# The gate's last product, made whole behind its own block or by quarters inside the next one

## The chip, the core and the metric

One core of a Trainium2 chip runs the whole kernel. The metric is the device time of one execution in microseconds (us), given as the median of several runs. Traces are of one profiled execution each; times inside a trace are counted from the first instruction of the span.

## What is computed

The layer takes x of shape 8 x 256 x 512 and returns `x + s * g`. `xn` is x with each row normalized; `s` is a latent attention over xn, `g` is the silu of a small FFN over the same xn:

```python
xn = _layernorm(x, axis=-1)
s = _L0_attn_ref(xn, ...)                      # 128 heads, latent 64, rope part 64
gate = silu(_qlora_linear(xn, w1q, a1, b1))    # 512 -> 1376
up = _qlora_linear(xn, w3q, a3, b3)
g = silu(_qlora_linear(gate * up, w2q, a2, b2))  # 1376 -> 512
x = x + s * g

def _qlora_linear(x, wq, A, B):
    w = jnp.tile(wq, (1, 4))
    return x @ w.T + (x @ A.T @ B.T) * 0.5
```

The weights `wq` are tiled four times along the input. So the input can be folded, its four quarters summed, before it meets the weight. For the last product this means that the 1376 hidden features are folded to 344 ahead of the product with `w2q`. The low-rank part (A, then B) is carried along as two further rows of the folded input.

## The kernel before

The kernel has two phases. The first (`first_phase`, about the first 217 us of the trace) normalizes x, makes the small projections that attention needs and the whole FFN, and stores the gates `g` in DRAM. The second is attention. All instructions are issued in the order written: nothing reorders them across a queue, and each engine works its queue off in that order. PSUM tiles come from one pool of eight banks (`bank`), each reused when the engines have done with it.

The first phase goes over four token blocks `tb` of 512 tokens (L674). For each block:

- Six steps `u` (L676) call `main(tb, u)`, which handles two of the eleven hidden chunks (one in the last step). For each chunk TensorE makes `px` and `py`, four matmuls of 32 x 512 each (`on_columns`, L169). VectorE adds the low-rank part (L541 and L545), ScalarE applies silu (L544), and the product gate times up is made on GpSimd (L558) or VectorE (L551, L552, L556). The gate tiles have two buffers.
- `fold` (L560) sums the four quarters of the hidden features on GpSimd (L570 to L572) into `h4`, in three parts; parts 1 and 2 come behind step 5. `low_out` (L574) makes the low-rank part `pm2` on TensorE. Its third call finishes it: ScalarE (L592) and three VectorE instructions (L594) write it into rows 96 to 127 of the third part of `h4`.
- If there is a next block, its transposes come in step 4, and behind step 5 come `sums` (L474: L479 on VectorE, L480 on GpSimd, L481 on VectorE), `narrow` (TensorE `pm`, then L497 on VectorE and copies L505 on ScalarE), the third `low_out` of this block, and `down` (TensorE `pp`). VectorE's L594 stands behind L481 and L497 in its queue, and L480 behind the folds in GpSimd's.
- `gate_out(tb)` (L598, called at L711) makes the last product. For each of four tiles of 128 tokens, a bank `pf` collects three parts k of `h4` times `w2_sb`, each four matmuls. The order is: parts 0 and 1 of all four tiles, then part 2 of all four. Part 2 is the one that waits for L594. ScalarE then takes each bank with a silu into a tile `gs` (L608; two buffers), and SyncE's queue stores it (L609), 256 KB each.
- Behind it come a set-up (tb = 0 only) and the statistics of the block after the next (`norm`, L715: VectorE L416 to L430, GpSimd L440 to L450). ScalarE's `norm_one` uses them in the steps of the next block.

`h4` has one buffer. The last block (tb = 3) has pieces of attention's projections (`Project`, L679) placed in its steps 2 to 5, and preparations (`between`) behind each step; there `gate_out(3)` is the last work on TensorE before attention begins.

The core of the last product before the change:

```python
for ks in ((0, 1), (2,)):
    for n in range(4):
        for k in ks:
            on_columns(
                pfs[n], h4s[tb][:, k, ds(n * P, P)], w2_sb[:, k, :], k == 0, k == 2
            )
```

Of the kernel before, what the change touches and what calls it, by code (L numbers as in the profile page):

```python
# [37 lines left out]
def mla_ffn_gate_kernel(  # L38
# [60 lines left out]
    def bank(name):  # L99
        return ps_all.tile([P, 512], F32, tag="b", name=name)  # L100
# [68 lines left out]
    def on_columns(to, w, x, start, stop):  # L169

        for t in range(4):
            tile_ = slice(32 * t, 32 * t + 32)
            nc.tensor.matmul(to[tile_], w[:, tile_], x, start=start, stop=stop, skip_group_check=True)  # L173
# [140 lines left out]
    def first_phase(between):  # L314
# [16 lines left out]
        def load_x(tb):  # L331
            xts[tb] = []
            for n in range(4):
                t = f1.tile([P, D], F32, tag="xt", name=f"xt_{tb}_{n}", bufs=6)
                nc.sync.dma_start(out=t, in_=x[ds(tb * TB + n * P, P), :])
                xts[tb].append(t)
# [116 lines left out]
        def norm_one(tb, n, mv, rstd, off):  # L453
            xns[tb] = xts[tb]
            xn, one = xts[tb][n], rstd[:, n : n + 1]
            if tb:
                nc.scalar.activation(xn, xn, AF.Identity, bias=off[:, n : n + 1], scale=one)
            else:
                nc.vector.tensor_scalar(xn, xn, mv[:, n, 0:1], one, ALU.subtract, ALU.mult)

        def turn(tb):
            a = f1.tile([P, KT, TB], F32, tag="act1", name=f"act1_{tb}")
            xnT[tb] = a
            for n in range(4):
                pt = bank(f"xpt_{tb}_{n}")
                for c in range(KT):
                    nc.tensor.transpose(pt[:, ds(c * P, P)], xns[tb][n][:, ds(c * P, P)], ident)
                pt = pt.rearrange("p (c s) -> p c s", c=KT)
                if tb or n % 2 == 0:
                    nc.scalar.copy(a[:, 0:KT, ds(n * P, P)], pt)  # L470
                else:
                    nc.vector.tensor_copy(a[:, 0:KT, ds(n * P, P)], pt)
# [38 lines left out]
        def down(tb):  # L511
            c = f1.tile([P, TB], F32, tag="tmp", name=f"c_{tb}")
            nc.scalar.copy(c, over_xn(tb, "pp", wdn_sb))
            nc.sync.dma_start(out=cs_d[tb], in_=c)
            sum_x(tb, xnT[tb])
# [3 lines left out]
        def pair(u):  # L519


            return [2 * (i % 4) + i // 4 if i < 8 else i for i in range(2 * u, min(2 * u + 2, NCH))]

        def place(c):
            return 4 * (c % 2) + c // 2 if c < 8 else c

        def main(tb, u):

            n = u // 2
            if u % 2 == 0:  # L530
                hTs[tb, n] = f2.tile([P, 4, TB], F32, tag="hT", name=f"hT_{tb}_{n}")
            h = hTs[tb, n]
            chunks = pair(u)
            gates, ups = [], []
            for i, c in enumerate(chunks):
                px, py = (bank(f"p{'xy'[k]}_{tb}_{u}_{i}") for k in range(2))
                on_columns(px, w1_sb[:, c], xsum[tb][0], True, True)
                on_columns(py, w3_sb[:, c], xsum[tb][1], True, True)
                gates.append(f2.tile([P, TB], F32, tag="gate", name=f"gate_{tb}_{u}_{i}"))
                ups.append((py, h[:, c // 2, :] if c < 8 and (tb or u > 1) and (i == 0 or u in (0, 2)) else py))  # L540
                nc.vector.scalar_tensor_tensor(  # L541
                    gates[i], lows[tb][0], bcol_sb[:, place(c), 0:1], px, ALU.mult, ALU.add
                )
                nc.scalar.activation(gates[i], gates[i], AF.Silu)  # L544
                nc.vector.scalar_tensor_tensor(  # L545
                    ups[i][1], lows[tb][1], bcol_sb[:, place(c), 1:2], py, ALU.mult, ALU.add
                )
            for c, gate, (py, up) in zip(chunks, gates, ups):
                if c >= 8:
                    m = c - 8  # L550
                    nc.vector.tensor_mul(h[0:96, m, :], gate[0:96], py[0:96])  # L551
                    nc.vector.tensor_mul(  # L552
                        h[32 * m : 32 * m + 32, 3, :], gate[96:128], py[96:128]
                    )
                elif up is py:
                    nc.vector.tensor_mul(h[:, c // 2, :], gate, py)  # L556
                else:
                    nc.gpsimd.tensor_mul(up, gate, up)  # L558

        def fold(tb, n):  # L560

            rows = CH[n][1]
            h = hTs[tb, n]
            if n == 0:
                h4s[tb] = f1.tile([P, 3, TB], F32, tag="h4", name=f"h4_{tb}")
            if n == 2:
                nc.gpsimd.memset(h4s[tb][64:96, n, :], 0.0)
            h4 = h4s[tb][:rows, n, :]
            h4b = f1.tile([P, TB], F32, tag="h4b", name=f"h4b_{tb}_{n}")
            nc.gpsimd.tensor_add(h4, h[:rows, 0, :], h[:rows, 1, :])  # L570
            nc.gpsimd.tensor_add(h4b[:rows], h[:rows, 2, :], h[:rows, 3, :])  # L571
            nc.gpsimd.tensor_add(h4, h4, h4b[:rows])  # L572

        def low_out(tb, n):  # L574


            rows = CH[n][1]
            h = hTs.pop((tb, n))
            if n == 0:
                mid2ps[tb] = bank(f"pm2_{tb}")  # L580
            for q in range(4):
                nc.tensor.matmul(
                    mid2ps[tb][32 * q : 32 * q + 32, :],
                    a2_sb[:rows, q, n, :],
                    h[:rows, q, :],
                    start=(n == 0),
                    stop=(n == 2),
                )
            if n == 2:
                m2 = mid2ps.pop(tb)  # L590
                to = h4s[tb][96:128, n, :]
                nc.scalar.mul(to, m2[0:32], 0.5)  # L592
                for q in range(1, 4):
                    nc.vector.scalar_tensor_tensor(  # L594
                        to, m2[32 * q : 32 * q + 32], 0.5, to, ALU.mult, ALU.add
                    )

        def gate_out(tb):  # L598
            pfs = [bank(f"pf_{tb}_{n}") for n in range(4)]
            for ks in ((0, 1), (2,)):  # L600
                for n in range(4):
                    for k in ks:
                        on_columns(
                            pfs[n], h4s[tb][:, k, ds(n * P, P)], w2_sb[:, k, :], k == 0, k == 2
                        )
            for n in range(4):
                gs = f2.tile([P, D], F32, tag="gs", name=f"gs_{tb}_{n}")
                nc.scalar.activation(gs, pfs[n], AF.Silu)  # L608
                nc.sync.dma_start(out=gates_d[4 * tb + n], in_=gs)  # L609
# [64 lines left out]
        for tb in range(NTB):  # L674
            more = tb + 1 < NTB
            for u in range(6):  # L676
                pj = None
                if not more and u >= 2:
                    pj = Project(u - 2)  # L679
                    pj.start()  # L680
                main(tb, u)
                if pj:
                    pj.second()
                    pj.end()
                if u in (3, 5):
                    fold(tb, u // 2 - 1)
                    low_out(tb, u // 2 - 1)
                if u == 1 and tb == 0:
                    stats = norm(1)
                if more:  # L690
                    for n in range(4):
                        if u == (n if tb else 2 + n // 2):
                            norm_one(tb + 1, n, *stats)
                if u == 4 and more:
                    turn(tb + 1)
                if u == 1 and tb + 2 < NTB:
                    load_x(tb + 2)
                if tb == NTB - 2 and u == 1:
                    between(1)
                if u == 5:  # L700
                    fold(tb, 2)
                if not more:
                    between(u + 2)
            if more:
                sums(tb + 1)
                narrow(tb + 1)
                low_out(tb, 2)
                down(tb + 1)
            else:
                low_out(tb, 2)  # L710
            gate_out(tb)  # L711
            if tb == 0:
                between(0)
            if tb + 2 < NTB:
                stats = norm(tb + 2)  # L715
# [42 lines left out]
    def between(step):  # L758
# [25 lines left out]
        else:  # L784
# [3 lines left out]
            load_act(3)  # L788

    first_phase(between)  # L790


# [330 lines left out]
```

## Time and profile before

| what | value |
|---|---|
| median of 3 runs | 1985.15 us (1983.88 to 1985.93) |
| the profiled execution's own time | 1985.59 us |
| its span, first to last instruction | 1983.8 us |
| mean granted TensorE clock | 0.998 |
| busy share of the span: TensorE, VectorE, ScalarE, GpSimd | 99%, 79%, 55%, 38% |
| first `px` of block 0, 1, 2, 3 | 23.61, 69.69, 113.17, 155.57 us |
| first score matmul of attention behind `gate_out(3)` | 217.01 us |

The profile names engines PE (TensorE), DVE (VectorE), ACT (ScalarE), POOL (GpSimd), and SPq for the DMA queue that SyncE issues into. In a timeline a row has the start, the duration, the engine, the line of the code, the operation, what it writes and reads, and how many instructions were merged; in square brackets is the idle time just ahead of it and what ended it. Each four matmuls of `on_columns` appear as eight records. Matmuls overlap, so their pace is read from the starts of successive groups: `px` at 113.17 us, `py` at 114.03, `px` at 114.89 make 0.86 us for four matmuls of 512 columns. A table by windows gives, for stretches of time, each engine's busy time and the number of instructions, the granted TensorE clock (PEclk; 1.00 is full speed), and the DMA share.

### The profile page before, as it was taken

Reading aid. Unit: us, or ns where it says so; the run is one execution under the profiler, and the core shown is the slowest. Engines: PE = TensorE matmul, PEld = TensorE weight load, DVE = VectorE, ACT = ScalarE, POOL = GpSimd, SP = SyncE. Lnnn points to the kernel's source line nnn. Section 1 sums busy time; section 2 is a strip of 40 time slices with the busy share of each in tenths; the row PEclk is TensorE's granted clock in tenths of the full one; section 3 lists DMA queues with packets and bytes.
Section 4 is the critical chain, followed back from the end, with each engine's and each line's share of the span. In section 5 each row is a group of like instructions: output and inputs, shape, how many; then the busy total and the mean of one; then the engine's idle time right before and its main releaser. Section 6 shows DMA issues by size and latency. Waiting matters only on the chain.

```text
span 1983.8 us, 86720 instructions
## 1 busy us (share of the span) xinstructions
PE 1966.9 (99%) x38065; PEld 1401.4 (71%) x38065; DVE 1571.2 (79%) x2666; ACT 1091.4 (55%) x2987; POOL 759.1 (38%) x1113
## 2 busy tenths in 40 slices
PE   8999999999999999999999999999999999999998
PEld 4334577777777767777777767777777767777776
DVE  7764678888787877788787877788787877888788
ACT  3333556556556555556556555556556555556654
POOL 5876545554552323232232323232332323232231
PEclk9999999999999999999999999999999999999999
DMA  6235322222232223221232223221232222222212
GB/s 195 100 118 184 109 88 87 88 69 85 88 129 74 100 87 111 91 87 66 87 117 76 100 87 108 93 88 66 88 115 77 100 87 86 83 88 84 70 56 71
DMA packets 120049, 187.53 MB, mean 95 GB/s; under 512 B 10716, under 2 KB 84844, under 8 KB 119674
## 3 DMA queue, kind: packets, MB, share of 16 engines
q1 hardware_dynamic: 119665, 181.97, 26.8%
q8 instruction: 301, 4.93, 1.0%
q14 instruction: 75, 0.61, 0.1%
q10 hardware_dynamic: 8, 0.02, 0.0%
HBM read 147.86 MB, written 34.10 MB: 92 GB/s over the span
## 4 chain that ended last, share of the span: by engine, by line
PE 91%; POOL 3%; DVE 3%; issue 2%; DMA 1%; ACT 0%; SPq 0%; POOLq 0%; ACTq 0%; DVEq 0%
PE q L173 40%; PE sc L824 34%; PE av L870 11%; PE po L173 2%; PE pf L173 1%; PE qq L249 1%; DVE pt L853 1%; POOL hT L558 1%; POOL h4b L571 0%; DVE nmx L837 0%; POOL h L570 0%; PE py L173 0%; DMA xt<-in_x_dram 0%; PE px L173 0%; POOL h L572 0%
## 5 line engine op out<-in xcount | busy, mean ns | idle before, releaser
L843 ACT ACTIVATE pr<-sc,nmx 128x256 f32<-128x256 f32 x2048 | 814.4, 500 | 471.8 <-DVE nmx L837 469.0
L837 DVE TENSOR_REDUCE nmx<-sc 128x2 f32<-128x512 f32 x1024 | 635.6, 683 | 288.9 <-PE sc L824 264.8
L853 DVE STREAM_TRANSPOSE pt<-pr 128x512 f32<-128x512 f32 x1024 | 635.1, 678 | 0.0
L216 POOL TENSOR_TENSOR e<-e,e 128x256 f32<-128x256 f32 x128 | 93.8, 733 | 1043.8 <-ACT e L211 558.2
L173 PE MATMUL q<-x,ws 128*32 128x256 f32 x8192 | 488.9, 379 | 0.2 <-POOL ws L137 0.2
L824 PE MATMUL sc<-act,qr 32*128 32x256 f32 x8192 | 488.6, 374 | 0.0
L824 PEld LDWEIGHTS sc<-act,qr 32*128 32x128 f32 x8192 | 421.0, 185 | 21.9 <-issue 0.2
L173 PEld LDWEIGHTS q<-x,ws 128*32 128x32 f32 x8192 | 266.1, 110 | 176.3 <-POOL ws L137 0.6
L173 PE MATMUL q<-x,w 128*32 128x256 f32 x6144 | 381.6, 381 | 0.7 <-DVE py L545 0.7
L173 PEld LDWEIGHTS q<-x,w 128*32 128x32 f32 x6144 | 187.0, 110 | 155.8 <-ACT pr L843 35.9
L824 PE MATMUL sc<-kc,qcm 32*128 32x256 f32 x4096 | 280.9, 387 | 0.0
L870 PE MATMUL av<-pt,vpad 128*32 128x128 f32 x8192 | 236.4, 273 | 1.9 <-ACT pr L843 1.2
L870 PEld LDWEIGHTS av<-pt,vpad 128*32 128x32 f32 x8192 | 226.4, 110 | 14.5 <-issue 3.0
L824 PEld LDWEIGHTS sc<-kc,qcm 32*128 32x128 f32 x4096 | 198.2, 184 | 51.9 <-issue 39.4
L211 ACT COPY e<-q 128x256 f32<-128x256 f32 x512 | 202.3, 396 | 25.5 <-PE q L173 25.3
L890 ACT ACTIVATE acc<-av,sides_sb 128x256 f32<-128x256 f32 (+1 forms) x130 | 54.2, 469 | 246.6 <-PE av L870 246.6
L269 POOL TENSOR_TENSOR qcm<-qc,mask_sb 128x1024 f32<-128x1024 f32 x64 | 122.3, 1911 | 0.0
L217 POOL TENSOR_TENSOR e<-e,e 128x256 f32<-128x256 f32 x128 | 93.6, 732 | 10.0
L218 POOL TENSOR_TENSOR qr<-e,e 128x256 f32<-128x256 f32 x128 | 93.6, 731 | 10.1
L310 POOL COPY vpad<-vall 32x128 f32<-32x128 f32 x256 | 74.9, 292 | 10.7 <-PE av L870 2.7
L228 DVE TENSOR_TENSOR qr<-e,q 128x256 f32<-128x256 f32 x128 | 53.9, 421 | 22.5 <-POOL e L216 17.0
L541 DVE SCALAR_TENSOR_TENSOR gate<-low,bcol_sb,px 128x512 f32<-128x512 f32 x44 | 32.8, 745 | 43.6 <-POOL hT L558 24.5
(124 smaller groups left out, 1134.5 us busy)
## 6 DMA issues: line engine op xcount, KB each, us to landing
w<-in_w_rope_dram SPq DMA_DIRECT2D x128, 512.0 KB
ws<-sums_d SPq DMA_DIRECT2D x96, 512.0 KB
sums_d<-ws SPq DMA_DIRECT2D x32, 512.0 KB
x<-xs_d SPq DMA_DIRECT2D x28, 256.0 KB
xt<-in_x_dram SPq DMA_DIRECT2D x16, 256.0 KB
xs_d<-xt SPq DMA_DIRECT2D x16, 256.0 KB
gate_d<-gs SPq DMA_DIRECT2D x16, 256.0 KB
g<-gate_d SPq DMA_DIRECT2D x16, 256.0 KB
```

Source lines behind the costliest of these rows:

```text
L173: nc.tensor.matmul(to[tile_], w[:, tile_], x, start=start, stop=stop, skip_group_check=True)
L211: nc.scalar.copy(self.e[i], self.banks[i])
L216: nc.gpsimd.tensor_add(m6, m6, m1)
L217: nc.gpsimd.tensor_add(m7, m7, m6)
L218: nc.gpsimd.tensor_add(self.out(1, 1), self.split(m7), self.split(m5))
L269: nc.gpsimd.tensor_mul(qcm, qks[b, sg // 2][0].rearrange("p (q i) -> p q i", i=32).unsqueeze(2).to_broadcast([P, 8, 4, 32]), mask_sb[:, ds ...
L310: nc.gpsimd.tensor_copy(vpad[rows, :, :, 8 * t + 4 * (sg % 2) :][..., :4], valls[b][rows, :, sg])
L824: nc.tensor.matmul(sc[r][:, h, :], lhs.rearrange("p t i -> p (t i)"), rhs, start=(part == 0 and h == 0), stop=(part == 2), skip_group_chec ...
L837: nc.vector.tensor_reduce(nmx[:, r, :], scs[n, f][r], AX.X, ALU.max, negate=True)
L843: nc.scalar.activation(p[:, h, :], scs[n, f][r][:, h, :], AF.Exp, bias=nmxs[n, f][:, r, h : h + 1])
L853: nc.vector.transpose(pts[n, f // 2, r].rearrange("p k q i -> p q k i")[:, ds(2 * (f % 2), 2)], prs.pop((n, f, r)).rearrange("p h (k j) -> ...
L870: nc.tensor.matmul(av[32 * r : 32 * r + 32, ds(half * P, P)], vpad[:, k, r, :], pt[r][:, k].rearrange("p q i -> p (q i)"), start=(k == 0), ...
```

## The change

`gate_out` takes the list of tiles that it makes. For blocks 0 to 2 it is no longer called behind the block. In its place, each of the steps u = 0 to 3 of the next block calls it for one tile, in front of that step's `main`. For the last block it stays where it was, with all four tiles.

```diff
-        def gate_out(tb):
-            pfs = [bank(f"pf_{tb}_{n}") for n in range(4)]
+        def gate_out(tb, tiles):
+            pfs = {n: bank(f"pf_{tb}_{n}") for n in tiles}
             for ks in ((0, 1), (2,)):
-                for n in range(4):
+                for n in tiles:
                     for k in ks:
                         on_columns(
                             pfs[n], h4s[tb][:, k, ds(n * P, P)], w2_sb[:, k, :], k == 0, k == 2
                         )
-            for n in range(4):
+            for n in tiles:
                 gs = f2.tile([P, D], F32, tag="gs", name=f"gs_{tb}_{n}")
                 nc.scalar.activation(gs, pfs[n], AF.Silu)
                 nc.sync.dma_start(out=gates_d[4 * tb + n], in_=gs)
@@
                     pj = Project(u - 2)
                     pj.start()
+                if tb and u < 4:
+                    gate_out(tb - 1, [u])
                 main(tb, u)
@@
             else:
                 low_out(tb, 2)
-            gate_out(tb)
+                gate_out(tb, range(4))
             if tb == 0:
                 between(0)
```

On TensorE's queue the order at a block's end was: `pp`, parts 0 and 1 of tiles 0 to 3 (32 matmuls), part 2 of tiles 0 to 3 (16 matmuls), then the next block's first `px`. Now it is: `pp`, parts 0, 1, 2 of tile 0 (12 matmuls), the next block's four products of step 0, then 12 matmuls of tile 1, step 1, and so on. ScalarE's four silus and SyncE's four stores of a block move with them; the orders on VectorE and GpSimd are the same as before.

## The prediction

> **What bounds the kernel now.** I read the page first: PE is busy almost all the time at full clock, so what counts is PE's time and any hole in it.
>
> ```profile
> span 1983.8 us, 86720 instructions
> PE 1966.9 (99%) x38065; PEld 1401.4 (71%) x38065; DVE 1571.2 (79%) x2666; ACT 1091.4 (55%) x2987; POOL 759.1 (38%) x1113
> ```
>
> The change touches only the first 217 us, so I next cut that stretch at the first `px` of blocks 1, 2, 3 and at attention's first matmul (table by windows: PE, PEld, DVE, ACT, POOL busy, granted clock, DMA).
>
> ```profile
> 69.69:113.17 43.48, 41.90 (x412) 14.72 (x408) 30.12 (x49) 17.00 (x28) 31.84 (x44) 1.00 0.33 115
> 113.17:155.57 42.40, 41.38 (x413) 14.63 (x408) 26.57 (x38) 17.01 (x28) 29.31 (x35) 1.00 0.39 132
> 155.57:217.01 61.44, 59.89 (x908) 26.23 (x900) 26.43 (x41) 19.57 (x42) 47.23 (x57) 1.00 0.42 148
> ```
>
> PE holds the pace here too; the holes are small. Then the timelines around the ends of blocks 0 and 1, PE first.
>
> ```profile
> 58.98 7.05 PE L173 MATMUL pf<-w_sb,h 128*32 128x512 f32 x64
> 66.26 2.31 PE L173 MATMUL pf<-w_sb,h 128*32 128x512 f32 x17 [0.23 <-issue]
> ...
> 102.39 7.05 PE L173 MATMUL pf<-w_sb,h 128*32 128x512 f32 x64
> 109.74 3.64 PE L173 MATMUL pf<-w_sb,h 128*32 128x512 f32 x32 [0.30 <-DVE h L594]
> 113.17 1.07 PE L173 MATMUL px<-xs,w_sb 128*32 128x512 f32 x8
> ```
>
> The 64 records of parts 0 and 1 run while part 2 is not ready; part 2 starts as soon as L594 is done. DVE's rows say when that is, and why:
>
> ```profile
> 64.01 2.14 DVE L594 SCALAR_TENSOR_TENSOR h<-pm,h 32x512 f32<-32x512 f32 x3 [1.99 <-ACT h L592]
> ...
> 98.05 1.10 DVE L479 TENSOR_TENSOR xs<-act 128x512 f32<-128x512 f32 x1
> 102.92 1.76 DVE L481 TENSOR_TENSOR xs<-xs,xs 128x512 f32<-128x512 f32 x1 [3.77 <-POOL xs L480]
> 107.46 2.14 DVE L594 SCALAR_TENSOR_TENSOR h<-pm,h 32x512 f32<-32x512 f32 x3 [1.99 <-ACT h L592]
> ```
>
> So part 2 comes at the end of a chain: folds on POOL, L480, L481, L497, copies on ACT, L594. The long first piece of `gate_out` is what PE does meanwhile. Last, ACT, where the old order has its cost:
>
> ```profile
> 118.98 1.23 ACT L608 ACTIVATE gs<-pf 128x512 f32<-128x512 f32 x2 [6.65 <-DMA gate_d<-gs]
> 120.23 1.15 ACT L544 ACTIVATE gate<-gate 128x512 f32<-128x512 f32 x2
> ```
>
> The third `gs` waits 6.65 us for a buffer still being stored. The silus of step 0 stand behind it, then POOL's products, then VectorE's step 1.
>
> **What moves, on PE.** Nothing is added: 12 groups (0.86 us each, 10.3 us) per block either way. What changes is what stands ahead of the part that waits.
>
> Block 0 to 1: up to `pp` all is as before, so L594 ends at 66.15 as before. PE has done tile 0's parts 0 and 1 (16 records at 0.107 us, 1.72) at 60.70, and must then wait to 66.26 with everything queued behind: tiles 1 to 3, and step 0's `px`. Hole 5.56 us, where 0.41 was lost (58.98 + 6.87 = 65.85). The first `px` comes at 67.12 instead of 69.69, but three tiles (7.72 us) are still owed.
>
> Block 1: PE's work to the next wait is 0.86 (tile 0, part 2), 13.7 (steps 0 to 3, 16 groups), 7.7 (tiles 1 to 3), 3 `low_out` 2.6, step 4 3.4, transposes 2.2, step 5 1.7, `pm` 3.5, `pp` 3.4, tile 0's parts 0 and 1 1.7: 40.8. No wait is in sight: the silus of step 0 no longer stand behind the stores, and VectorE's step 1 starts at 77.8 (POOL's set-up ends at 76.45, plus one 1.3 us product), 2 us earlier than before. So PE is there at 66.26 + 40.8 = 107.05. L594: PE now reaches step 3 late, `px` of step 4 goes at 89.4, and VectorE follows PE. Step 4 on VectorE starts at 90.5 (89.59 before), its four products end at 96.65, and step 5's end at 99.5 (98.02 before). POOL's second add of the last fold (L571) waits for that: 99.55 + 1.72, L572 and L480 to 103.85 (102.88 before). From L480 to L594 it was 102.88 to 109.60, 6.72 us; so L594 ends at 110.6. Hole 3.6 us, where 0.48 was lost. The next `px` is at 111.5 (113.17 before).
>
> Block 2 has no set-up, but the same PE pace from step 2 on: again 44.4 us from hole end to hole end, 110.7 to 155.0, hole 3.6 us (0.45 before), first `px` of block 3 at 155.9 (155.57 before).
>
> Block 3 then has 7.72 us more PE work than before.
>
> The sum: holes 5.56 + 3.6 + 3.6 = 12.8, less the 1.3 lost there now: +11.4. What the change gives back: block 1 took 43.48 for 40.8 of work, 2.6 lost, of which 0.48 is in the hole: 2.1 (waits for banks behind `gs` and behind the late VectorE). Block 2: 42.40 for 40.6, less 0.45: 1.35. Block 3: `py` at 161.97 waits for `gs`, and `q` at 167.40 for L545, 0.9 each; I take 1.5. Together 5.0. Net +6.4 us.
>
> **Other queues.** ACT: silus of a tile are 0.60 us, one per step, and ACT is under half busy there: hidden; the second one waits behind `norm_one` for POOL's offsets to 77.3 in block 1, but the bank it frees is wanted at 80.8. SP: four stores per block, 0.5 to 1.3 us of issue each. The loads of x for the block after the next, and in block 2 the loads of rope weights, now stand behind two stores instead of four, so not later. In block 3, tile 1's store stands behind the two stores of `ws`, which wait for POOL (168.7 and 171 before); the silu that needs its buffer is wanted near 186. Were that cover gone, tile 3's silu would be late and a bank with it: 3 us at most. Banks: `pf` now is one of five per step, not four; in block 3, with `Project`'s four, nine are wanted of eight, and the ninth takes a bank that ACT has copied out by then: between the last of `Project`'s first products and that group lie 2.6 us of `pf` and three groups, 5 us of PE work. No gain is seen there and at most 1 us of loss; I take 0. After attention starts nothing moves relative to `gate_out(3)`; PE has no slack there (its waits of over 0.3 us behind 217 us sum to under 2 us), so the shift arrives whole at the end.
>
> **The rule that weighs.** No PE wait in this trace is longer than 1.7 us behind the first 12 us, so no row shows what a 5.56 us hole does to the clock. The nearest rows are at the start: the clock falls in 8.5 to 9.0 and comes back at about 15.5, almost 7 us at half, although PE idles only 1.45 us there (its earlier work was transposes and two-row products).
>
> ```profile
> 8.50:9.00 0.50, 0.50 (x2) 0.70 1.01 286
> 9.00:9.50 0.50, 0.50 (x2) 0.50 1.24 217
> 15.00:15.50 0.50, 0.50 (x12) 0.50 0.31 86
> 15.50:16.00 0.50, 0.50 (x16) 0.97 0.85 225
> ```
>
> The Trainium skill, "TensorE: Matmul & The Clock Gate", section "Why this matters for your kernels", asks for no idle gaps over about 3 us between bursts, since an idle window puts the clock to half until a busy one has passed; Part 1 gives a free-running window of about 3.4 us. By the rows of full speed alone a hole costs only itself (+6.4). By the rule, a drop costs one window at half, an estimate of 1.7 us (up to 3.4 if it lasts the 7 us of the start's rows). A hole of 5.56 holds an empty window in (5.56 - 3.4)/3.4, some 60 cases of 100 and more if a nearly empty one is enough; a hole of 3.6 seldom. I take one drop, at the first hole: +1.7.
>
> **Forecast.** 6.4 + 1.7 = +8.1 us. The profiled execution would have a span of 1983.8 + 8.1 = 1991.9 and a time of 1985.59 + 8.1 = 1993.7 (1.8 us lie outside the span); from the median, 1985.15 + 8.1 = 1993.3.
>
> **Rivals.**
> - No drop of the clock: 1985.15 + 6.4 = 1991.6. For it: 3.6 us holes are at the edge and the first may straddle two windows.
> - Drops at all three holes, 1.7 to 2.6 each: 6.4 + 5.1 to 7.8, 1996.7 to 1999.4.
> - A buffer or bank wait in block 3 on top: 1993.3 + 3 = 1996.3.
> - Not slower: holes 2 and 3 close, because L594 in blocks 1 and 2 ends before PE comes to tile 0's part 2, at 107.05 or earlier and not 110.6. Then 5.56 - 1.34 - 5.0 = -0.8: 1984.4. For it: VectorE is freed 2 us earlier in step 1. Against: from step 3 on VectorE waits for PE's `px`, so the early start is lost, and POOL's last fold cannot start its second add before step 5's products. If the two holes together are under 4.3 us instead of 7.2, the sum is still within 0.2%. The first hole remains in any case: nothing ahead of it changes.
>
> **Numbers.** Forecast 0.42, no drop 0.26, three drops 0.10, extra wait 0.06, not slower 0.16 (0.13 within 0.2%, which is about what a measurement of this kernel can tell from no change, and 0.03 faster). Slower therefore 0.84. The range leaves out the best half of the last case and the worst of the three-drop one: 1988.0 to 1998.0.
>
> **What would show it.** PE idle of about 5.5 us from 60.7 with L594 as releaser, then 3 to 4 us near 107 and 151; ACT's 6.65 us wait for `gate_d` gone; first `px` of blocks 1, 2, 3 near 67, 111.5 to 113, 156 to 158; PEclk under 1.00 behind 66 us if it dropped; first score matmul near 223.5 to 225. Wrong if L594 ends by 107 in block 1, or if VectorE starts step 4 of block 1 well ahead of 90.

## The result, and the profile after

| | before | after |
|---|---|---|
| median of 5 runs each, side by side | 1985.15 us (1983.72 to 1985.93) | 2000.14 us (1998.21 to 2001.9) |
| ratio after to before, 95% interval | | 1.0073 (1.0063 to 1.0084) |
| the profiled execution's own time | 1985.59 us | 2000.75 us |
| its span | 1983.8 us | 1999.0 us |
| mean granted TensorE clock | 0.998 | 0.993 |
| part 2 of tile 0 starts, end of block 0, 1, 2 | 66.26, 109.74, 152.14 us | 66.10, 113.00, 160.34 us |
| first score matmul | 217.01 us | 231.66 us |

The changed kernel is 15.0 us slower; 8.1 had been forecast, and the time lies outside the range. The head of its page shows the same instructions as before, and 7.3 us more busy time on PE although it has no more work:

```profile
span 1999.0 us, 86720 instructions
PE 1974.2 (99%) x38065; PEld 1403.2 (70%) x38065; DVE 1572.9 (79%) x2666; ACT 1092.2 (55%) x2987; POOL 759.0 (38%) x1113
```

PE's timeline at the ends of blocks 0, 1 and 2 says why. Each end now has one tile's parts 0 and 1 (16 records, 1.7 us), then a hole, then part 2:

```profile
58.85 1.90 PE L173 MATMUL pf<-w_sb,h 128*32 128x512 f32 x16
66.10 1.94 PE L173 MATMUL pf<-w_sb,h 128*32 128x512 f32 x8 [5.34 <-issue]
67.77 1.97 PE L173 MATMUL px<-xs,w_sb 128*32 128x512 f32 x8
69.48 1.68 PE L173 MATMUL py<-xs,w_sb 128*32 128x512 f32 x8
...
107.37 1.90 PE L173 MATMUL pf<-w_sb,h 128*32 128x512 f32 x16
113.00 1.93 PE L173 MATMUL pf<-w_sb,h 128*32 128x512 f32 x8 [3.74 <-DVE h L594]
114.68 1.96 PE L173 MATMUL px<-xs,w_sb 128*32 128x512 f32 x8
...
154.71 1.90 PE L173 MATMUL pf<-w_sb,h 128*32 128x512 f32 x16
160.34 1.93 PE L173 MATMUL pf<-w_sb,h 128*32 128x512 f32 x8 [3.73 <-DVE h L594]
162.02 1.96 PE L173 MATMUL px<-xs,w_sb 128*32 128x512 f32 x8
```

Two things are to be read. The holes (in square brackets): 5.3, 3.7 and 3.7 us. And the durations behind them: a group of four matmuls (8 records) takes 1.9 us where it took 1.07 before, and the next group starts 1.7 us later, not 0.86. That is the clock. The table by windows shows each hole and the stretch of five groups behind it (length; busy time of PE, PEld, DVE, ACT, POOL; granted clock; DMA share; GB/s):

```profile
60.00:66.00 6.00, 0.75 (x8) 0.00 (x0) 3.91 (x5) 3.02 (x5) 5.92 (x13) 0.83 0.22 48
66.10:72.69 6.59, 6.59 (x41) 1.89 (x45) 5.86 (x15) 1.23 (x2) 6.04 (x28) 0.65 0.95 338
109.10:113.00 3.90, 0.17 (x4) 0.03 (x1) 2.18 (x4) 2.12 (x4) 2.43 (x2) 0.83 0.28 90
113.00:120.03 7.03, 7.03 (x40) 1.95 (x44) 5.65 (x14) 1.23 (x2) 2.25 (x12) 0.61 0.99 352
156.50:160.34 3.84, 0.11 (x4) 0.03 (x1) 2.07 (x3) 2.05 (x4) 2.36 (x2) 0.89 0.28 91
160.34:167.60 7.26, 7.26 (x40) 1.83 (x40) 2.11 (x3) 1.23 (x2) 0.96 (x1) 0.59 0.98 349
```

Behind each hole PE is busy without a break, at a mean clock of about 0.6. Five groups at full speed are 5 x 0.86 = 4.29 us; they took 6.59, 7.03 and 7.26, so the clock cost 2.30 + 2.74 + 2.97 = 8.0 us in this execution. The page's mean clock agrees: 0.002 x 1983.8 = 4.0 us were lacking before and 0.007 x 1999.0 = 14.0 after, 10 us more, of which some 2 us fall on time in which PE idled anyway. It was one of the executions that lost most: the five were granted 0.993, 0.993, 0.997, 0.996 and 0.994. So 8.0 us is the price in the profiled execution, and the median may hold less of it: by their mean, 0.9946, some 11 us were lacking in place of 14.

When the clock fell and rose is seen in windows of 1 us around the first hole (length; busy time of PE alone; granted clock; DMA share; GB/s):

```profile
63.00:64.00 1.00, 0.00 (x0) 0.96 0.05 12
64.00:65.00 1.00, 0.00 (x0) 0.50 0.28 70
...
69.00:70.00 1.00, 1.00 (x8) 0.50 1.00 342
70.00:71.00 1.00, 1.00 (x12) 0.63 1.02 371
71.00:72.00 1.00, 1.00 (x16) 1.00 1.02 377
```

0.96 over one microsecond means that it fell at 63.92, and 0.63 that it rose at 70.74, 6.8 us later. The same reckoning gives 111.7 to 118.5 for the second hole and 159.5 to 166.3 for the third.

The chain that releases part 2 has its old form. At the first hole it ends at 65.99 us, though the row of part 2 names no releaser ("issue"); at the second it comes later than before, with the waits for the folds (3.76 us) and for ScalarE (1.99 us) of before:

```profile
63.85 2.14 DVE L594 SCALAR_TENSOR_TENSOR h<-pm,h 32x512 f32<-32x512 f32 x3 [1.99 <-ACT h L592]
...
106.19 1.75 DVE L481 TENSOR_TENSOR xs<-xs,xs 128x512 f32<-128x512 f32 x1 [3.76 <-POOL xs L480]
...
110.72 2.14 DVE L594 SCALAR_TENSOR_TENSOR h<-pm,h 32x512 f32<-32x512 f32 x3 [1.99 <-ACT h L592]
```

And ScalarE's wait of 6.65 us for a buffer is gone; the silus of a block come one by one:

```profile
68.09 0.60 ACT L608 ACTIVATE gs<-pf 128x512 f32<-128x512 f32 x1 [3.66 <-PE pf L173]
...
76.99 0.57 ACT L608 ACTIVATE gs<-pf 128x512 f32<-128x512 f32 x1
...
81.52 0.60 ACT L608 ACTIVATE gs<-pf 128x512 f32<-128x512 f32 x1 [0.57 <-PE pf L173]
```

### The profile page after: what moved, and what is told of

It reads as the page before. It is cut to its first block, busy times and chain, and to the rows that moved or that the text cites. A ratio compares the mean times of both kernels' runs of the same rounds, so it can differ in the third digit from the quotient of the medians.

```text
span 1999.0 us, 86720 instructions
## 1 busy us (share of the span) xinstructions
PE 1974.2 (99%) x38065; PEld 1403.2 (70%) x38065; DVE 1572.9 (79%) x2666; ACT 1092.2 (55%) x2987; POOL 759.0 (38%) x1113
## 4 chain that ended last, share of the span: by engine, by line
PE 94%; DVE 3%; POOL 2%; issue 1%; ACT 0%; DMA 0%; SPq 0%; POOLq 0%; ACTq 0%; DVEq 0%
PE q L173 39%; PE sc L826 34%; PE av L872 11%; PE po L173 2%; PE pf L173 2%; PE px L173 1%; PE py L173 1%; PE qq L249 1%; DVE pt L855 1%; DVE nmx L839 0%; POOL h4b L571 0%; PE vps L294 0%; POOL xt L158 0%; POOL h L570 0%; DMA xt<-in_x_dram 0%
```

## The experiments

The theory after the result: the change loses the holes (12 us) and three falls of the clock (8 us), and gains what the stall of the silus had cost (5 us). The first rival: the slow groups behind the holes are not the clock's doing but come from contention, for the DMA share is 0.95 to 0.99 there. The second: what is gained comes from moving the products, not from the silus and their buffers. The runs were made in three groups, each on one chip with its own runs of the kernel before: 1986.9 us (first), 1985.78 (second), 1986.48 (third). Each time is set against that of its group.

### Filling the holes

Only extra work on TensorE, into a bank that nobody reads, put where PE waits. What is waited for stays the same; the hole does not.

```diff
             for ks in ((0, 1), (2,)):
+                if ks == (2,) and len(tiles) == 1 and tiles[0] == 0:
+                    idle = bank(f"fill_{tb}")
+                    for i in range((6, 4, 4)[tb]):
+                        on_columns(idle, h4s[tb][:, 0, ds(0, P)], w2_sb[:, 0, :], True, True)
                 for n in tiles:
```

**6, 4 and 4 groups of four matmuls (first group of runs).**

> The changed kernel with idle work put into its three holes: in front of part 2 of tile 0, TensorE makes 6, 4 and 4 extra groups of four matmuls (0.86 us a group, into a bank that nobody reads; their results are left out of the output). The order of everything else is that of the changed kernel. Theory (holes plus clock): the waits for L594 cost 12.0 us net of what was lost before, the half clock behind each of them 2.3 + 2.7 + 3.0 = 8.0 us, and 4.8 us are given back elsewhere. With the holes filled the granted clock stays at 1.00 and only the 8.0 us go: 2000.1 - 8.0 = 1992.1 us, range 1991 to 1993.5. Rival (the 7 us beyond the forecast come from the quarters themselves, by banks or a longer chain, and the clock only accompanies them): the time stays at 1998 to 2002 even though the clock is at 1.00.

Measured: 1996.57 us, ratio 1.0054 (1.0042 to 1.0067), +9.7 over before: outside the expected range and outside the rival's, a miss. The clock stayed at full speed (0.998 over the span, as before). From one end of the wait to the next it is 44.6 us (66.36 to 110.98 to 155.59), where the changed kernel took 46.9 and 47.3: the 2.3 and 2.7 us that were put down to the clock. So contention for DMA is out: behind the three filled holes the DMA share is nearly as high as in the changed kernel, and PE's clock is at 1.00, with groups 0.86 us apart (table by windows, columns as above):

```profile
66.40:72.00 5.60, 5.60 (x56) 2.06 (x60) 5.33 (x15) 1.23 (x2) 5.28 (x24) 1.00 0.94 330
111.50:117.40 5.90, 5.90 (x60) 2.11 (x56) 5.63 (x15) 1.73 (x3) 1.82 (x10) 1.00 0.91 315
156.00:162.00 6.00, 6.00 (x84) 2.18 (x80) 2.99 (x4) 2.56 (x5) 2.25 (x2) 1.00 0.99 351
```

But the time fell by less than the 8 us. One part of that is a wait that appeared in block 3 and that no other row explains:

```profile
174.78 2.78 PE L173 MATMUL pf<-w_sb,h 128*32 128x512 f32 x24 [1.90 <-issue]
```

**The changed kernel once more, in the third group**, as a base for the next three.

> The changed kernel itself once more, on the same chip as the three kernels with filled holes of this group, so that these can be set against it directly. 15 us slower than the kernel before (13 to 16), three falls of the granted clock to 0.50, each of one or two windows of 3.4 us.

Measured: 1999.62 us, ratio 1.0067 (1.0054 to 1.0079), +13.1; waits ending at 66.43, 112.98 and 160.13 us, three falls again, which by the same five groups cost 1.9 + 2.6 + 2.9 = 7.4 us.

**6, 4 and 4 again.**

> The fill by 6, 4 and 4 groups again under a name of this group, beside the changed kernel. Its first profile had blocks 1 and 2 faster than the changed kernel by 2.3 and 2.7 us, just what the half clock had cost there, but a wait of 1.9 us in block 3 that no other row explains. Theory (holes plus clock): 5.5 to 8 us faster than the changed kernel, the more of the 8.0 the less that wait shows. Rival (the clock is absorbed elsewhere): under 4 us faster than the changed kernel.

Measured: 1996.44 us, 1.0051 (1.0039 to 1.0064): 3.2 us under the changed kernel, a miss, and what the rival had (under 4). Again no fall of the clock, waits ending at 66.57, 111.17 and 155.79, and again a wait in block 3 at the same group:

```profile
174.36 2.78 PE L173 MATMUL pf<-w_sb,h 128*32 128x512 f32 x24 [1.28 <-ACT e L211]
```

**5, 4 and 3.**

> Fill by 5, 4 and 3 groups, which leaves holes of at most 1.3 us and meets block 3 with TensorE's queue in another phase. Theory: as the fill by 6, 4 and 4: no fall of the clock, 5.5 to 8 us faster than the changed kernel. Rival for the wait of 1.9 us in block 3 (it belongs to the last of four fill groups): gone here, and the time 1.9 us under that of the other fill.

Measured: 1994.06 us, 1.0038 (1.0024 to 1.0051): 5.6 us under the changed kernel, at the lower end of what was expected, and +7.6 over before. The first hole is short now, and behind it the groups run at full speed; in block 3 the wait is absent:

```profile
59.57 1.90 PE L173 MATMUL pf<-w_sb,h 128*32 128x512 f32 x16
61.28 4.47 PE L173 MATMUL fill<-w_sb,h 128*32 128x512 f32 x40
66.83 1.07 PE L173 MATMUL pf<-w_sb,h 128*32 128x512 f32 x8 [1.07 <-issue]
67.68 1.07 PE L173 MATMUL px<-xs,w_sb 128*32 128x512 f32 x8
...
173.17 3.08 PE L173 MATMUL pf<-w_sb,h 128*32 128x512 f32 x24
```

This is the kernel as the forecast had it without the clock: the intervals are 44.6, 44.6 and 68.7 us (to the first score matmul at 224.78), where the forecast said 44.4, 44.3 and 68.5. The wait of 0 to 2 us in block 3 stays open: the two fills differ in nothing but the number of extra matmuls, and the profile names no releaser in one trace and in the other a copy on ScalarE that had ended 0.6 us before (173.79 us). The trace of the changed kernel itself hasn't got it.

Where the rest of the 8 us went is seen when the trace is cut at the first score matmul. From the start of the first hole's `pf` to there it was 172.8 us in the changed kernel (58.85 to 231.66) and 165.2 here (59.57 to 224.78): 7.6 us less, against the 8.0 put down to the clock. The two runs with 6, 4 and 4 took 167.0 and 166.4; without the wait in block 3 both come to 165.1. But behind the first score matmul, where nothing differs, the kernels with extra matmuls took 1768.0 to 1770.0 us against 1767.3, and no run says why.

**1 group each: holes shorter, not gone.** This asks how short a hole must be.

> Fill by one group at each hole, which leaves about 4.7, 2.9 and 2.9 us. In earlier runs a hole of 2.8 us made the clock fall and holes of 2.0 us did not. Theory (a window of 3.4 us with under about a third of it busy makes it fall): it falls at all three, and no time is saved against the changed kernel (within 2 us). Rival (only holes over 3.4 us make it fall): it falls at the first alone, 4 to 5.5 us faster than the changed kernel.

Measured: 2001.51 us, 1.0074 (1.0061 to 1.0087), 1.9 us over the changed kernel, as the theory had it (within 2 us), though the profiled execution's span (1997.6) is 1.3 under its (1998.9). No gain, at any rate: holes of 4.49, 2.88 and 2.86 us, and the clock fell at all three. The second one, in windows of 1 us on PE:

```profile
111.00:112.00 1.00, 0.30 (x4) 1.00 0.88 238
112.00:113.00 1.00, 1.00 (x12) 0.91 0.85 305
113.00:114.00 1.00, 1.00 (x8) 0.50 1.01 349
...
116.00:117.00 1.00, 1.00 (x13) 0.89 1.03 379
```

It fell at 112.8, when PE was already at work for 1.1 us. So "only holes longer than 3.4 us" is wrong.

**3, 2 and 2 groups (first group of runs).**

> As the fill by 6, 4 and 4 groups, but with 3, 2 and 2: the holes are left at about 5.5 - 2.6 = 2.9, 1.9 and 1.9 us. In the changed kernel the clock fell in windows of 3.4 us in which TensorE was busy 0.25 to 0.8 us. Theory, that a nearly idle window is what makes it fall: no window of the second and third hole has under 1.3 us of work, so it falls at most at the first: 1992.1 to 1994.5 us. Rival, that any window that isn't nearly full makes it fall (after a fall, windows with 2.3 to 2.6 us of work did not bring it back): three falls as before, 1998 to 2001 us.

Measured: 1996.11 us, 1.0049 (1.0035 to 1.0062), over the expected 1994.5; against its own group it is +9.2, where the range came to +7.0 to +9.4. Holes of 2.79, 2.02 and 2.00 us; the clock fell at the first alone and rose 3.4 us later, and not at those of 2.0:

```profile
110.00:111.00 1.00, 0.93 (x12) 1.00 0.00 0
111.00:112.00 1.00, 0.00 (x0) 1.00 0.33 119
112.00:113.00 1.00, 0.06 (x4) 1.00 0.72 231
113.00:114.00 1.00, 1.00 (x12) 1.00 0.84 291
```

### Letting the late operand come earlier

`low_out`'s third call, with L592 and L594, ahead of the sums and of `narrow`, so that part 2 no longer waits behind them:

```diff
-                sums(tb + 1)
-                narrow(tb + 1)
-                low_out(tb, 2)
+                pm = over_xn(tb + 1, "pm", ck_sb)
+                low_out(tb, 2)
+                sums(tb + 1)
+                narrow(tb + 1, pm)
                 down(tb + 1)
```

> The changed kernel, quarters and all, but the third low-rank part is finished (L592, L594) ahead of the sums of the next block (L479, L481) in the queues of ScalarE and VectorE, with the pm product still ahead of it on TensorE. Nothing is left out. Theory (the price is where part 2 waits, not that the product is cut in quarters): part 2 is then ready when TensorE comes to it; what is left is a wait of the first px for the copies L505, about 1.9, 1.0 and 1.0 us, no fall of the clock, and the 5.0 us given back stay: 1985.15 + 3.9 - 1.3 - 5.0 = 1982.7 us, range 1980.5 to 1985. Rival (the interleaving itself is costly, since products of two blocks share eight banks): no better than with filled holes, 1990 or more.

Measured: 1990.15 us, ratio 1.0019 (1.0012 to 1.0027): 10 us better than the change and still slower than before, a miss. The rival's figure (1990 or more) was met, but the trace shows other causes than the shared banks that it named. Tile 0's product now runs in one piece (24 records), and the next in line waits: the first `px`, for the folded x that comes down the same chain (L507 and L505 of the kernel before are the same copies).

```profile
58.41 2.76 PE L173 MATMUL pf<-w_sb,h 128*32 128x512 f32 x24
63.42 1.79 PE L173 MATMUL px<-xs,w_sb 128*32 128x512 f32 x8 [2.25 <-ACT xs L507]
...
150.71 1.07 PE L173 MATMUL px<-xs,w_sb 128*32 128x512 f32 x8 [1.90 <-ACT xs L507]
```

The hole of 2.25 us let the clock fall for 3.4 us (63.6 to 67.0), those of 1.90 and 1.91 did not. To judge by the mean clock it did not do so in each execution: the six of the fifteen that were granted 0.999 took 1987.5 to 1989.9 us, the six that were granted 0.997 took 1990.9 to 1994.7. And PE came to block 3 so early that a round trip through DRAM, which used to be covered, showed: VectorE waited there for `low`, stored and loaded again.

```profile
155.50 0.75 DVE L543 SCALAR_TENSOR_TENSOR gate<-low,bcol_sb,px 128x512 f32<-128x512 f32 x1 [5.55 <-DMA low<-low_d]
```

From its first `px` to the first score matmul (220.74) block 3 took 70.0 us, where the kernel with 5, 4 and 3 extra groups took 67.9 (156.93 to 224.78): 2.2 us lost. With the 5.0 given back taken from the forecast, the whole comes to 6.1 (holes) + 1.7 (clock) + 2.2 - 1.3 (waits of before) - 5.0 = 3.7 us, and the first score matmul is 3.7 us later than before (217.01).

### The gain without the loss

**The kernel before, with more buffers for the silus** (tiles 2 and 3 use two tiles of another tag that are free by then); no matmul is moved.

```diff
-                gs = f2.tile([P, D], F32, tag="gs", name=f"gs_{tb}_{n}")
+                gs = f2.tile([P, D], F32, tag="gs" if n < 2 else "mid", name=f"gs_{tb}_{n}")
```

> The kernel before, last product whole and behind its own block, but tiles 2 and 3 of gs take the buffers of mid in place of waiting for the stores of tiles 0 and 1. Nothing is left out. Theory: the wait of 6.65 us of ScalarE for a gs buffer is what held up the silus of step 0 and cost TensorE 2.1 + 1.35 + 1.5 us in the three blocks behind it; without it most of these come back: 1985.15 - 4 = 1981.2 us, range 1979.9 to 1983. Rival (TensorE's small waits there have other causes, POOL's norm chain or the banks of pf): within 1 us of 1985.15.

Measured: 1980.81 us, ratio 0.9971 (0.9961 to 0.9982): 6.1 us faster than before, the largest gain of all, within the expected range (against its own group it is a little above that range, which came to 2.2 to 5.3 us). Its interval overlaps those of the two kernels below. ScalarE's rows show the third and the fourth `gs` without the wait of 6.65 us:

```profile
110.99 0.60 ACT L608 ACTIVATE gs<-pf 128x512 f32<-128x512 f32 x1 [0.26 <-PE pf L173]
111.90 0.60 ACT L608 ACTIVATE gs<-pf 128x512 f32<-128x512 f32 x1 [0.31 <-DMA xs_d<-act]
```

and on PE the long first piece still covers the wait for part 2:

```profile
100.82 7.05 PE L173 MATMUL pf<-w_sb,h 128*32 128x512 f32 x64
108.15 3.64 PE L173 MATMUL pf<-w_sb,h 128*32 128x512 f32 x32 [0.28 <-DVE h L594]
111.58 1.07 PE L173 MATMUL px<-xs,w_sb 128*32 128x512 f32 x8
```

**Parts 0 and 1 of all tiles behind the block, part 2 with silu and store by quarters.** A new `gate_most` holds the first piece:

```diff
+            gate_most(tb)
...
                 if tb and u < 4:
                     gate_out(tb - 1, [u])
```

> Parts 0 and 1 of all four tiles behind their own block as in the kernel before (they are what TensorE does while L594 is late), and only part 2, silu and store of each tile in front of the next block's steps 0 to 3. Nothing is left out. Theory: the price of the change is the work taken out of that wait; with it back there are no holes over 0.5 us and no half clock, and the gain that the change was seen to make elsewhere (4.8 us, from the silus that no longer wait for the stores) stays, less about 1 us for four pf banks held over the steps: 4 us faster than the kernel before, range 2.5 to 5.5. Rival (cutting the product over the steps costs by itself, in banks or on ScalarE): no faster than the kernel before.

Measured: 1981.94 us, ratio 0.9982 (0.9975 to 0.999), -3.8 us, within the range. PE waits 0.22 us at part 2 of block 0 and not at all at the next two.

**The whole product behind the block, silus and stores alone by quarters.**

```diff
+            gate_product(tb)
...
         def gate_out(tb, tiles):
             for n in tiles:
                 gs = f2.tile([P, D], F32, tag="gs", name=f"gs_{tb}_{n}")
```

> The whole product behind its own block as in the kernel before, with only the silus and stores one by one in front of the next block's steps 0 to 3. Nothing is left out. Theory: as for the part-2 split, ScalarE's wait for gs buffers is gone and TensorE keeps its cover: 4.5 us faster than the kernel before, range 3 to 6.5 (the kernel with more gs buffers was 6.1 us faster on its chip). Rival (the silus one by one hold the pf banks, so that TensorE waits for them): within 1 us of the kernel before.

Measured: 1981.59 us, ratio 0.998 (0.9973 to 0.9987), -4.2 us, within the range. So the second rival falls: the gain is there without a single product moved.

**The split, and `low_out` early as well.**

> The part-2 split, and L592 and L594 ahead of the next block's sums in their queues. Nothing is left out. Theory: part 2 of tile 0 no longer waits at all (0.41 to 0.48 us at each of three block ends), and parts 0 and 1 of the four tiles, 6.9 us, still cover the copies into xs and most of the round trip of low through DRAM: 1 us better than the part-2 split, 5 us faster than the kernel before, range 3 to 6.5. Rival (the early L594 moves the sums and the first px back, as it did with the quarters): no better than the part-2 split, or slower.

Measured: 1982.0 us, ratio 0.9981 (0.9974 to 0.9987), -3.8 us. No more than the split alone, as the rival had it: once the 6.9 us of first pieces cover the wait, an earlier L594 can only take away those 0.22 us.

### Quarters at the end of block 0 alone

```diff
-                if tb and u < 4:
+                if tb == 1 and u < 4:
                     gate_out(tb - 1, [u])
...
                 low_out(tb, 2)
+            if tb:
                 gate_out(tb, range(4))
```

> Quarters only at the first block end (block 0's product inside block 1); blocks 1 to 3 keep theirs whole behind them. Nothing is left out. Theory (each block end pays for itself): hole 5.5 for 0.4, half clock 2.3, given back in block 1 2.2: 5.2 us slower than the kernel before, range 4 to 6.5, with a granted clock of 0.50 for about 4.5 us behind the hole and nowhere else. Rival (the three block ends only cost together, because each delays the next chain): under 3 us slower, as later whole products swallow the delay.

Measured: 1988.83 us, ratio 1.0017 (1.001 to 1.0023), +3.05 us: below the range that was expected, and just above the rival's 3. The hole was as long (5.36 us), but this time the clock was at half for 3.4 us only, from 66.1 to 69.5, of which PE worked 2.7, and that cost 1.3 us instead of 2.3:

```profile
66.85 1.93 PE L173 MATMUL pf<-w_sb,h 128*32 128x512 f32 x8 [5.36 <-issue]
68.53 1.55 PE L173 MATMUL px<-xs,w_sb 128*32 128x512 f32 x8
69.89 1.05 PE L173 MATMUL py<-xs,w_sb 128*32 128x512 f32 x8
```

The ends of the later blocks have their cover: at block 1 all 96 records run in one piece without a wait, at block 2 the 64 first records stand before part 2 and the wait is 0.29 us. In its profile the first score matmul comes at 221.24 us, 4.2 later than before; 0.6 of that lies ahead of the hole (its `pf` starts at 59.60, not 58.98), where nothing differs. The other 3.6 are hole 5.1 more than before and clock 1.3, less 2.9: 0.5 for the wait at block 1's end that is gone, and 2.4 given back elsewhere, for which the forecast had 2.1. The medians differ by 3.05, 0.6 less than 3.6. So later blocks swallow at most the 0.5, not the delay itself.

## Why the prediction was wrong in size and right in direction

| term | predicted | measured | from |
|---|---|---|---|
| holes beyond those of before | +11.4 | +12.0 | starts of part 2: 5.53 + 3.91 + 3.91, less 1.34 |
| half clock | +1.7 | +8.0 | the five groups behind each hole |
| given back | -5.0 | -5.2 | blocks 1, 2, 3: 2.3 + 1.3 + 1.7, from part 2 to part 2 (to the first score matmul in block 3), less hole, clock and moved work |
| elsewhere | 0 | +0.4 | 0.5 behind the first score matmul, less 0.1 ahead of the first hole |
| sum | +8.1 | +15.2 | spans 1983.8 and 1999.0 us |

**The step that failed** is "a hole of 3.6 seldom. I take one drop, at the first hole: +1.7". There were three drops, and each cost more than the 1.7 of one window. The rival with drops at all three holes, 1996.7 to 1999.4 us at a chance of 0.10, was nearest; the upper end of its price, 2.6 us a hole, was about the mean of what was measured (2.7).

Two assumptions stood behind that step. The first was that a window must be empty, or nearly so, for the clock to fall. It need not be. Falls and rises lie 3.4 or 6.8 us apart in every trace looked at, and from a rise to the next fall it was 41.0 us twice in the changed kernel (70.74 to 111.70, 118.53 to 159.49), twelve times 3.41. So I take windows of 3.41 us in a row with these instants and count PE's work in each, behind the first 57 us and ahead of attention:

| PE's work in the window | what the clock did at its end | kernels and holes |
|---|---|---|
| 0 to 0.99 us (0 to 29%) | fell | changed kernel (0.25, 0.98, 0.54); the same again, first and third; one extra group, first; quarters at block 0 alone |
| 1.12 to 1.16 us (33 to 34%) | fell | 3, 2, 2 groups, first; one extra group, second; early `low_out`, first |
| 1.34 and 1.37 us (39 and 40%) | fell | changed kernel again, second; one extra group, third |
| 1.51 to 1.65 us (44 to 48%) | stayed at full speed | early `low_out`, second and third; the wait in block 3 with 6, 4, 4 groups, first run |

A hole of 2.25 us was enough when it lay so; those of 1.9 to 2.0 us, whose windows were 44% busy at the least, did not make it fall. The second assumption was that one window at half speed ends it. The window after the fall still holds the rest of the hole: it was 1.2, 2.1 and 2.6 us busy (36 to 75%), and that did not bring the clock back, so a second window was served, 6.8 us in all. With one extra group 2.6 us (76%) did not suffice at the third hole and 2.67 us (78%) did at the first; with the quarters at block 0 alone 2.69 us (79%) did. So the price of a hole ran from 1.3 to 3.0 us, by where it lay.

Busy time is not the whole rule: at the start of every trace, where PE ran transposes and two-row products, a window that was 55 to 100% busy was followed by a fall, so the shares above are shown only for the products behind it.

The Trainium skill, "TensorE: Matmul & The Clock Gate", section "Why this matters for your kernels", warns of gaps over about 3 us and speaks of one idle window. Its warning held for the holes of 3.7 us, and the estimate drawn from it read "idle" too strictly; the runs go further than the page, since 2.25 us sufficed in a window that was one third busy, and the measurement decides. The start of the kernel's own trace had shown almost 7 us at half beside 1.45 us of idling. The prediction named it as an upper price and then took the lower.

**What held.** The first hole, with everything ahead of it unchanged: 5.56 forecast, 5.53 measured. The later ones: 3.6 forecast, 3.9 measured; with the clock taken out (5, 4 and 3 extra groups), the forecast's intervals are met within 0.3 us each. In block 1 VectorE's step 4 began at 92.75 (forecast 90.5) and L594 ended at 112.86 (forecast 110.6), each later by the 2.3 us of the clock behind the first hole. The first `px` of blocks 1, 2 and 3 came at 67.8, 114.7 and 162.0, not at 67, 111.5 to 113 and 156 to 158, and the half clock behind each hole accounts for the lag: 46.90 - 2.30 = 44.6 and 47.34 - 2.74 = 44.6 us from wait to wait, for 44.4 and 44.3 forecast. What is given back was sized rightly, block by block (2.1, 1.35 and 1.5 forecast); removed alone, the stall of the silus was worth 6.1 (more buffers), 4.2 (silus by quarters) and 3.8 (part 2 by quarters). Store queue, loads and banks cost nothing that can be seen: between the first hole and attention PE has no wait over 0.2 us in the changed kernel's trace beside the three holes.

**Left open.** From the first score matmul to the end it is 1767.3 us after and 1766.8 before, but 1768.9 with the early `low_out` and up to 1770.0 with extra matmuls; and the wait in block 3 told of above.

## What to carry to other kernels

A product that is cut so that its parts which can run early go away from in front of the one that waits loses its cover: look for what TensorE does during a wait before moving that work, and move what stalls (here silus and stores, or give them two more buffers) instead of what covers. A hole on TensorE costs its length and, when it leaves a window of 3.4 us with no more than about two fifths of work (in these traces), another 1.3 to 3 us of half clock behind it; filling it with matmuls that nobody reads gave 3 to 6 us back, in medians. Where a trace shows an effect at its upper price, though at another place, say why it should cost less at the place in question before choosing the lower price.

## What the runs showed of the hardware that was not expected

- Behind the first 57 us, the granted clock fell after windows of 3.41 us that were 0 to 40% busy, not only after empty ones, and not after those of 44% or more; it came back after windows that were at least 78% busy, not after those of 15 to 76%.
- The same hole of 5.4 us cost 2.3 us of half clock in one kernel and 1.3 in another whose start lay 0.7 us later (58.85 and 59.60): where the hole lies against the windows decides. With the early `low_out`, executions of one and the same kernel were granted 0.999 or 0.997.
- With 6, 4 and 4 extra groups far ahead of it a wait of 1.3 to 1.9 us stood in block 3, with 5, 4 and 3 none, and no releaser in the profile explains it; the medians of the two differ by 2.4 us, as much as an effect under study.
